# Edge layer: part of one term per block moved to ScalarE with a bias, and the correction sum formed in two steps

## The chip, the cores and the metric

The kernel runs on one core of one Trainium2 chip. The metric is the device time of one execution in microseconds. Each kernel is run several times and the median is compared. The core's engines run their own instruction streams side by side: PE (TensorE) multiplies matrices, DVE (VectorE), ACT (ScalarE) and POOL (GpSimd) work element by element, and SP issues transfers. SBUF is the on-chip memory, PSUM the small memory into which PE accumulates.

## The reference, cut to what matters

The program is a chain of four residual layers on a tensor of 4 images, 56 x 56 pixels, 128 channels. Each layer normalises its input by groups and adds its result to it. The change concerns layer 1 alone:

```python
def _L1_conv_ref(x, We, be, Wn, bn):
    f = x.shape[-1]
    W1, W2 = (We[:, :f], We[:, f:])
    proj_i = jnp.einsum('blnf,of->blno', x, W1)
    proj_j = jnp.einsum('blnf,of->blno', x, W2)
    edge = jax.nn.relu(proj_i[:, :, :, None, :] + proj_j[:, :, None, :, :] + be)
    edge_sum = edge.sum(axis=3)
    node_in = jnp.concatenate([x, edge_sum], axis=-1)
    node = jax.nn.relu(jnp.einsum('blnc,oc->blno', node_in, Wn) + bn)
    return node

x = x + _L1_conv_ref(_gn(x), L1_conv_We, L1_conv_be, L1_conv_Wn, L1_conv_bn)
```

For each image row l and each pixel n in it, the layer adds up relu(a[n] + b[m]) over all 56 pixels m of the same row, for 128 output channels. Here a is the first projection with its bias, and b the second. So there are 56 x 56 relus for each row and channel.

## The kernel before

The edge layer (`edge_layer`, from L1204) runs once for each image, between the attention and MLP of layer 0 for that image and the work that follows. Layers 2 and 3 come after all images, and the change doesn't touch them.

An image is cut into 7 blocks of 8 rows, that is 448 pixels (`NB`). The 56 pixels m are dealt out over the partitions: the 128 partitions hold 32 channels four times over, each time for another group of 14 pixels m, so that one "term" covers four pixels m at a time, and 14 terms (`M = HH // 4`) cover all 56. The 128 channels are cut into 4 quarters r of 32. A term is therefore a tile of 128 partitions x 4 quarters x 8 rows x 56 pixels, that is 128 x 1792 elements.

For each block, `project` lets PE compute four banks `e_pa` (first projection, one bank per quarter) and one bank `e_pc` (minus the second projection, 4 x 8 x 14 values). `evacuate` lets ACT copy them to SBUF as `e_a` (with the bias) and `e_c`, and adds the output bias to the residual. `normed` lets ACT normalise the input of the block after the next. With a in `e_a` and c = -b, the relu of a + b is relu(a - c), which is max(a, c) - c. Each term is made in one of three ways, by `terms` (L1265), which a string of one letter per term chooses:

- "d": DVE takes max(a, c) in one instruction (L1273), reading c from PSUM (`e_pc`). The missing "- c" is put in later, once for all d terms, by the correction.
- "p": POOL subtracts a - c (L1275), reading c from SBUF (`e_c`), and ACT applies the relu in place (L1277). No correction is needed.
- "s": a shared term. Quarters 0 and 1 are made as d, quarters 2 and 3 as p.

The letters stand in `EDGE_TURNS` for the first six blocks and in `EDGE_END` for the last. Before the change they are "ddpddpsdpdpddp" (8 d, 5 p, 1 s) and "ddpddpdpdpdddd" (10 d, 4 p).

PE then adds every term into the bank `e_acc`: four matmuls of 32 columns (L1344), one for each quarter, with a matrix that sums the four groups of partitions. The correction is a further set of four matmuls (L1360) with `e_rest`, which DVE makes by summing `e_c` over the d terms (L1366 and L1367). Where quarters 0 and 1 have one d term more than quarters 2 and 3, as with "s", the sum is taken in two instructions.

The order on PE, ACT and DVE is that of the program text (`tc.manual_schedule`). POOL's order is chosen by the framework from what the instructions depend on. In the text, at turn g the term is made and multiplied; then the finish of the block before last comes at g = 3 (`finish`, L1296, on DVE, which waits for PE's `e_po`), the first half of the next block's evacuation at g = 5, the second at g = 7, the sums for the correction at g = 8, the norm at g = 10 and the correction's matmuls at g = 11. After the last turn ACT copies the sums out of `e_acc` (L1369), and PE forms the output of the block before (`output`) and projects the block after the next.

Buffers: 7 tiles for d terms, 4 for p terms, 2 for each kind of partial tile. `e_a`, `e_c`, `e_rest` and `e_sums` have 2 each.

Of the kernel before, what the change touches and what calls it, by code (L numbers as in the profile page):

```python
# [12 lines left out]
F32 = mybir.dt.float32  # L13
AF = mybir.ActivationFunctionType
ALU = mybir.AluOpType
AX = mybir.AxisListType
# [3 lines left out]
P = 128  # L20
B = 4
HH = 56
# [10 lines left out]
def bc(ap, axis, n):  # L33

    ap = ap.unsqueeze(axis)
    shape = list(ap.shape)
    shape[axis] = n
    return ap.to_broadcast(shape)
# [1159 lines left out]

EDGE_TURNS, EDGE_END = "ddpddpsdpdpddp", "ddpddpdpdpdddd"


def edge_layer(k, w, x1, st):  # L1204
# [6 lines left out]
    nc, tc = k.nc, k.tc  # L1211
# [3 lines left out]
    with ExitStack() as es:  # L1215
        big = es.enter_context(tc.tile_pool(name="e_big", bufs=1))
        wk = es.enter_context(tc.tile_pool(name="e_wk", bufs=2))
# [7 lines left out]
        ready = {}  # L1225

        def normed(j):
            if j < 2:
                apply_norm(k, xg[:, blk(j)], xf[:, blk(j)], mr)
            elif j < NBLK:  # L1230
                nc.scalar.activation(xg[:, blk(j)], xf[:, blk(j)], AF.Identity, bias=shift, scale=mr[:, 1:2])
# [22 lines left out]
        def evacuate(j, part):  # L1254
            if j >= NBLK:
                return
            pc, pa, c, a = ready[j]
            for r in range(2 * part, 2 * part + 2):
                nc.scalar.activation(a[:, r, :], pa[r][:, :NB], AF.Identity, bias=w.be[:, r:r + 1])
                if r == 0:  # L1260
                    nc.scalar.copy(c.rearrange("p r l m -> p (r l m)"), pc[:, :NB])  # L1261
            if part == 1:
                nc.scalar.activation(xf[:, blk(j)], xf[:, blk(j)], AF.Identity, bias=w.bn)

        def terms(j, m, t, r0, r1, e):  # L1265

            pc, _, c, a = ready[j]
            if e == "d":
                c = pc[:, :NB].rearrange("p (r l m) -> p r l m", r=4, l=8)
            cm = bc(c[:, r0:r1, :, m], 3, HH)  # L1270
            am = a[:, r0:r1, :].rearrange("p r (l n) -> p r l n", l=8)
            if e == "d":
                nc.vector.tensor_tensor(t, am, cm, ALU.max)  # L1273
            else:
                nc.gpsimd.tensor_sub(t, am, cm)  # L1275
                tf = t.rearrange("p r l n -> p (r l n)")
                nc.scalar.activation(tf, tf, AF.Relu)  # L1277

        def tile_of(e, n=4):
            return wk.tile([P, n, 8, HH], F32, tag="e_%s%d" % (e, n), name="e_t" + e,  # L1280
                           bufs=2 if n < 4 else 7 if e == "d" else 4)
# [12 lines left out]
        def finish(j, po):  # L1294

            nc.vector.scalar_tensor_tensor(xf[:, blk(j)], po[:, :NB], w.nbn, xf[:, blk(j)], ALU.max, ALU.add)  # L1296

        with tc.manual_schedule(engines={mybir.EngineType.PE, mybir.EngineType.Activation, mybir.EngineType.DVE}):
            idle = psum.tile([P, 512], F32, tag="e_pc", name="e_idle", bufs=2)

            def fill(n):

                for _ in range(n):
                    nc.tensor.matmul(idle[:, :3 * P], k.ident, bc(k.ones, 1, 3), start=True, stop=True)
            mr = group_norm_factors(k, wk, bank, st, fill)
            nc.vector.tensor_scalar(shift, mr[:, 0:1], mr[:, 1:2], -1.0, ALU.mult, ALU.mult)
            for j in range(2):
                normed(j)
            project(0)
            for part in range(2):  # L1310
                evacuate(0, part)
            project(1)
            last = po = None
            for j in range(NBLK):
                end = j == NBLK - 1
                turns = EDGE_END if end else EDGE_TURNS
                nd, ns = turns.count("d"), turns.count("s")
                acc = psum.tile([P, 512], F32, name="e_acc")
                rest = wk.tile([P, 4, 8], F32, name="e_rest")
                at, ms = {"d": 0, "p": nd + ns, "s": nd}, []  # L1320
                for e in turns:
                    ms.append(at[e])
                    at[e] += 1
                early = {}
                if j == 0:
                    early = {g: tile_of(turns[g]) for g in
                             [g for g, e in enumerate(turns) if e == "d"][:3] + [turns.index("p")]}
                    for r in range(4):
                        for g, t in early.items():
                            terms(j, ms[g], t[:, r:r + 1], r, r + 1, turns[g])  # L1330
                for g, e in enumerate(turns):
                    m = ms[g]
                    if g in early:
                        parts = [(early[g], 0)]
                    elif e == "s":
                        parts = [(tile_of("d", 2), 0), (tile_of("p", 2), 2)]
                        for t, r in parts:
                            terms(j, m, t, r, r + 2, "p" if r else "d")
                    else:
                        parts = [(tile_of(e), 0)]  # L1340
                        terms(j, m, parts[0][0], 0, 4, e)
                    for t, r0 in parts:
                        for r in range(t.shape[1]):
                            nc.tensor.matmul(acc[quarters[r0 + r], :NB], w.S[:, 0, :], t[:, r].rearrange("p l n -> p (l n)"),  # L1344
                                             start=(g == 0), stop=(g == len(turns) - 1))
                    if g == 3 and po is not None:
                        finish(j - 2, po)
                    if g == 5:
                        evacuate(j + 1, 0)
                    if g == 7:  # L1350
                        evacuate(j + 1, 1)
                    if g == 10:
                        normed(j + 2)
                    if g == 6 and end:
                        po = output(*last)
                    if g == 9 and end:
                        finish(j - 1, po)
                    if g == 11:
                        for r in range(4):
                            nc.tensor.matmul(acc[quarters[r], :NB].rearrange("p (l n) -> p l n", l=8), w.S[:, 1, :],  # L1360
                                             bc(rest[:, r, :], 2, HH), start=False, stop=False)
                        if end:
                            po = begun(j)
                    if g == 8:
                        if ns:
                            nc.vector.tensor_reduce(rest[:, 0:2], ready[j][2][:, 0:2, :, 0:nd + 1], AX.X, ALU.add)  # L1366
                        nc.vector.tensor_reduce(rest[:, 2 if ns else 0:4], ready[j][2][:, 2 if ns else 0:4, :, 0:nd], AX.X, ALU.add)  # L1367
                sums = wk.tile([P, NB], F32, name="e_sums")
                nc.scalar.copy(sums, acc[:, :NB])  # L1369
                if end:  # L1370
                    idle = psum.tile([P, 512], F32, tag="e_pc", name="e_idle", bufs=2)
                    fill(2)
                if last and not end:
                    po = output(*last)
                project(j + 2)
                last = j, sums
            po = output(*last, po)
            fill(2)
            finish(NBLK - 1, po)
# [1476 lines left out]
def group_norm_factors(k, pool, bank, st, fill):  # L2856

    nc = k.nc
    mv = pool.tile([P, 2], F32, tag="mv", name="gf_mv")
    nc.vector.bn_aggr(mv, st.rearrange("p a b -> p (a b)"))  # L2860
    ps = bank()
    fill(2)
    nc.tensor.matmul(ps[:, 0:1], k.g4, mv[:, 0:1], start=True, stop=True)
    fill(1)
    mr = pool.tile([P, 2], F32, tag="mr", name="gf_mr")
    nc.vector.tensor_copy(mr[:, 0:1], ps[:, 0:1])
    t = pool.tile([P, 1], F32, tag="gt", name="gf_t")
    nc.vector.tensor_sub(t, mv[:, 0:1], mr[:, 0:1])
    nc.vector.tensor_mul(t, t, t)
    nc.vector.tensor_add(t, t, mv[:, 1:2])  # L2870
    ps = bank()
    nc.tensor.matmul(ps[:, 0:1], k.g4, t, start=True, stop=True)
    fill(1)
    nc.scalar.activation(t, ps[:, 0:1], AF.Sqrt, bias=k.eps)
    nc.vector.reciprocal(mr[:, 1:2], t)
    return mr
# [176 lines left out]
```

## Time and profile before

| | |
|---|---|
| median of 3 runs | 3447.18 us (3444.64 to 3448.79) |
| the profiled execution's own time | 3464.64 us |
| its span, first to last instruction | 3462.8 us |
| edge layer, first image: first DVE term | 544.46 us |
| edge layer, first image: end of the last DVE term | 673.31 us |
| starts of the sums copy (L1369), blocks 0 to 6 | 565.67, 583.91, 602.93, 620.73, 638.50, 655.72, 674.39 us |
| DVE, one whole term (L1273, 128 x 1792) | 2.01 us |
| POOL, one whole subtraction (L1275, 128 x 1792) | 3.28 us |
| POOL, two quarters / one quarter (L1275) | 1.74 / 0.95 us |
| ACT, relu of a whole term / two quarters / one quarter (L1277) | 1.71 / 0.96 / 0.57 us |
| DVE, the two correction sums (L1366, L1367) | 0.29, 0.27 us |

The four images' edge layers lie at about 541 to 677, 1175 to 1311, 1811 to 1947 and 2447 to 2583 us. Durations run from an instruction's start to its end. Instructions that follow each other on one engine overlap a little, so the time from start to start is shorter than the duration: a DVE term lasts 2.01 us, and the next starts 1.93 us after it.

### The profile page before, as it was taken

How to read it: one execution, taken by the hardware profiler on the slowest of the kernel's cores; microseconds unless marked ns; L12 is line 12 of the kernel's file. 1: busy time of each engine (PE TensorE's matmuls, PEld its weight loads, DVE VectorE, ACT ScalarE, POOL GpSimd, SP SyncE). 2: the span in 40 equal slices, each digit the busy share in tenths (PEclk: the TensorE clock that was granted, in tenths of full speed). 3: DMA queues.
4: the chain of work that ended last, by engine and by line, in shares of the span. 5: the costliest groups of instructions: out<-in, count | busy, mean ns of one | idle time of the engine just before them, and what ended most of it. 6: DMA issues, size and time to landing. Idle time of an engine off the chain costs nothing. (4 is left out here: it accounts for less than half of the span.)

```text
span 3462.8 us, 64536 instructions
## 1 busy us (share of the span) xinstructions
PE 3337.5 (96%) x27834; PEld 1441.2 (42%) x27834; DVE 2659.6 (77%) x2552; ACT 2134.9 (62%) x2257; POOL 1284.9 (37%) x795
## 2 busy tenths in 40 slices
PE   7999999999999999999999999999999999999998
PEld 4433333353333435333343443333337443346664
DVE  6588867868888696788859858887785878886756
ACT  4688876668888575788857568887654012215432
POOL 1000017700000490000019400001785978875766
PEclk9999999999999999999999999999999999999989
DMA  2243420024434000444310034342113057742201
GB/s 106 46 94 86 97 54 19 20 58 87 97 86 86 19 1 20 110 99 94 89 41 1 20 82 93 89 97 54 38 36 85 1 124 182 182 110 80 61 10 56
DMA packets 97868, 243.42 MB, mean 70 GB/s; under 512 B 64440, under 2 KB 69816, under 8 KB 92440
## 3 DMA queue, kind: packets, MB, share of 16 engines
q0 software_dynamic: 16128, 102.77, 14.8%
q1 hardware_dynamic: 74728, 123.61, 12.2%
q10 hardware_dynamic: 6720, 12.85, 1.3%
q8 instruction: 220, 3.60, 0.4%
q14 instruction: 72, 0.59, 0.1%
HBM read 79.43 MB, written 31.33 MB: 32 GB/s over the span
## 5 line engine op out<-in xcount | busy, mean ns | idle before, releaser
L830 ACT ACTIVATE f_ring<-f_pm 128x1792 f32<-128x1792 f32 (+1 forms) x764 | 1093.8, 1482 | 226.7 <-PE f_pm L827 179.2
L682 DVE TENSOR_TENSOR f_acc<-f_acc,f_ring 128x1792 f32<-128x1792 f32 x468 | 947.5, 2025 | 190.8 <-ACT f_ring L830 160.0
L827 PE MATMUL f_pm<-f_qT,f_kT 32*128 32x448 f32 x5376 | 722.8, 571 | 9.9 <-ACT f_p L716 4.1
L693 PE MATMUL f_pm<-f_ring,f_va 128*32 128x448 f32 (+1 forms) x6304 | 589.4, 490 | 0.0
L672 POOL DMA_DIRECT2D f_far<-f_ring x112 | 96.5, 862 | 1328.2 <-ACT f_ring L830 1027.0
L1275 POOL TENSOR_TENSOR e_tp<-e_a,e_c 128x1792 f32<-128x1792 f32 (+2 forms) x172 | 480.4, 2839 | 33.5 <-issue 33.4
L1273 DVE TENSOR_TENSOR e_td<-e_a,e_pc 128x1792 f32<-128x1792 f32 (+2 forms) x292 | 478.3, 1704 | 8.8 <-ACT e_c L1261 8.8
L827 PEld LDWEIGHTS f_pm<-f_qT,f_kT 32*128 32x128 f32 x5376 | 260.1, 183 | 411.8 <-ACT f_ring L830 301.1
L693 PEld LDWEIGHTS f_pm<-f_ring,f_va 128*32 128x32 f32 x6304 | 163.8, 109 | 410.1 <-issue 397.8
L1277 ACT ACTIVATE e_tp<-e_tp 128x1792 f32<-128x1792 f32 (+2 forms) x172 | 253.3, 1495 | 98.0 <-POOL e_tp L1275 98.0
L2040 DVE TENSOR_TENSOR u_ud<-u_px,u_d 112x1792 f32<-112x1792 f32 x144 | 263.4, 1863 | 39.9 <-PE u_po L2045 35.6
L2042 POOL TENSOR_TENSOR u_up<-xh,u_d 112x1792 f32<-112x1792 f32 (+1 forms) x72 | 240.9, 3374 | 56.0 <-PE u_po L2045 42.8
L1344 PE MATMUL e_acc<-e_td,t_edge 128*32 128x448 f32 x1952 | 231.6, 542 | 6.6 <-DVE e_td L1273 6.4
L2045 PE MATMUL u_po<-u_ud,AT 112*64 112x448 f32 x1056 | 212.4, 541 | 0.5 <-DVE u_ud L2040 0.5
L1344 PE MATMUL e_acc<-e_tp,t_edge 128*32 128x448 f32 x1184 | 148.0, 543 | 23.7 <-ACT e_tp L1277 23.6
L2045 PEld LDWEIGHTS u_po<-u_ud,AT 112*64 112x64 f32 x1056 | 74.0, 137 | 126.5 <-issue 112.3
L1344 PEld LDWEIGHTS e_acc<-e_td,t_edge 128*32 128x32 f32 x1952 | 61.8, 110 | 142.4 <-issue 94.2
L737 DVE RECIPROCAL f_den<-f_den 128x448 f32<-128x448 f32 x28 | 82.6, 2951 | 44.9 <-ACT f_den L734 44.9
L1874 POOL TENSOR_TENSOR q_u<-iS,q_g 128x1792 f32<-128x1792 f32 x32 | 104.3, 3287 | 12.2 <-PE q_acc L1889 12.2
L813 POOL TENSOR_TENSOR x<-xf,xw 128x343 f32<-128x343 f32 x28 | 25.5, 909 | 221.5 <-DVE xf L802 221.5
L2145 ACT COPY x_ev<-x_po 56x896 f32<-56x896 f32 x32 | 28.8, 900 | 126.7 <-DMA x_xs<-xat 57.8
L1889 PE MATMUL q_acc<-q_u,S 64*64 64x448 f32 x1024 | 101.2, 539 | 2.1 <-DVE y L1908 1.1
(538 smaller groups left out, 4622.3 us busy)
## 6 DMA issues: line engine op xcount, KB each, us to landing
f_far<-f_ring POOLq DMA_DIRECT2D x112, 896.0 KB, 6.4
u_d<-dd SPq DMA_DIRECT2D x46, 784.0 KB
f_far<-f_ring SPq DMA_DIRECT2D x28, 896.0 KB
xw<-in_x SPq DMA_DIRECT2D x4, 1568.0 KB
x2d<-x SPq DMA_DIRECT2D x4, 1568.0 KB
xat<-x SPq DMA_DIRECT2D x4, 1568.0 KB
x_xs<-xat ACTq DMA_DIRECT2D x32, 196.0 KB
xm<-x_ev ACTq DMA_DIRECT2D x64, 98.0 KB
```

The costliest lines, as they stand in the source:

```text
L682: nc.vector.tensor_add(e.acc, e.acc, slots(j, c))
L693: nc.tensor.matmul(e.po[heads[h], part], va[o, c, heads[h]], p, start=(c == 0), stop=(c == 23 and part.stop == NB))
L827: nc.tensor.matmul(ss[:, i, :NB], kT[heads[h], c * P:(c + 1) * P], qT[heads[h], blk(j)], start=True, stop=True)
L830: nc.scalar.activation(ring[:, slot:slot + m, :], ss[:, :m, :NB], AF.Exp, scale=scale)
L1273: nc.vector.tensor_tensor(t, am, cm, ALU.max)
L1275: nc.gpsimd.tensor_sub(t, am, cm)
L1277: nc.scalar.activation(tf, tf, AF.Relu)
L1344: nc.tensor.matmul(acc[quarters[r0 + r], :NB], w.S[:, 0, :], t[:, r].rearrange("p l n -> p (l n)"), start=(g == 0), stop=(g == len(turns) ...
L1874: nc.gpsimd.tensor_mul(u, bc(st.iS[:, bp, c, :HH], 1, HEADS), bc(g[:, n, c, :], 2, HH))
L2040: nc.vector.tensor_mul(u, bc(px[:, :, :NB], 2, m), dm)
L2042: nc.gpsimd.tensor_mul(u, bc(x, 2, m), dm)
L2045: nc.tensor.matmul(po[64 * b2:64 * b2 + 64, :NB], st.AT[:, 8 * i + h0 + q, 2 * bp + b2, :], u[:, b2, q, :], start=(left == 16), stop=(left ...
```

## The change

The letters become "ddpddpdpdpsddp" (still 8 d, 5 p, 1 s, with the s at turn 10 instead of 6) and, for the last block, "ddpddpdpdphddd" (9 d, 4 p, and one h at turn 10).

In a term "s" or "h", quarters 0 and 1 are now made by ACT alone: one activation for each of the 2 quarters x 8 rows, relu(a + bias) over 56 pixels, where the bias is a column of a small tile `e_less` that holds minus c. That makes 16 activations and one more for `e_less`, in four portions after turns 2, 4, 6 and 8. In "s", quarter 2 is made by DVE and quarter 3 by POOL and ACT. In "h", DVE makes quarters 2 and 3.

The correction is now one sum over the d terms for all four quarters, and one addition of the c of the shared term for the quarters that DVE made of it (one quarter in "s", two in "h").

```diff
-EDGE_TURNS, EDGE_END = "ddpddpsdpdpddp", "ddpddpdpdpdddd"
+EDGE_TURNS, EDGE_END = "ddpddpdpdpsddp", "ddpddpdpdphddd"
...
+        def singles(j, m):
+
+            t = tile_of("a", 2)
+            yield t
+            _, _, c, a = ready[j]
+            less = wk.tile([P, 2, 8], F32, name="e_less")
+            nc.scalar.activation(less, c[:, 0:2, :, m], AF.Identity, scale=-1.0)
+            for r in range(2):
+                for l in range(8):
+                    nc.scalar.activation(t[:, r, l, :], a[:, r, HH * l:HH * (l + 1)], AF.Relu, bias=less[:, r, l:l + 1])
+                    if l % 4 == 3:
+                        yield
...
-                nd, ns = turns.count("d"), turns.count("s")
+                nd, ns, nh = turns.count("d"), turns.count("s"), turns.count("h")
...
-                at, ms = {"d": 0, "p": nd + ns, "s": nd}, []
+                at, ms = {"d": 0, "p": nd + ns + nh, "s": nd, "h": nd}, []
...
+                work = singles(j, nd)
+                single = next(work)
...
-                    elif e == "s":
-                        parts = [(tile_of("d", 2), 0), (tile_of("p", 2), 2)]
-                        for t, r in parts:
-                            terms(j, m, t, r, r + 2, "p" if r else "d")
+                    elif e in "sh":
+                        parts = [(single, 0)]
+                        for e, r0, r1 in (("d", 2, 3), ("p", 3, 4)) if e == "s" else (("d", 2, 4),):
+                            parts.append((tile_of(e, r1 - r0), r0))
+                            terms(j, m, parts[-1][0], r0, r1, e)
...
+                    if g in (2, 4, 6, 8):
+                        next(work)
...
-                        if ns:
-                            nc.vector.tensor_reduce(rest[:, 0:2], ready[j][2][:, 0:2, :, 0:nd + 1], AX.X, ALU.add)
-                        nc.vector.tensor_reduce(rest[:, 2 if ns else 0:4], ready[j][2][:, 2 if ns else 0:4, :, 0:nd], AX.X, ALU.add)
+                        nc.vector.tensor_reduce(rest, ready[j][2][:, :, :, 0:nd], AX.X, ALU.add)
+                        r0, r1 = 2, 3 + nh
+                        nc.vector.tensor_add(rest[:, r0:r1], rest[:, r0:r1], ready[j][2][:, r0:r1, :, nd])
```

`ready[j][2]` is `e_c`, the copy of the second projection in SBUF.

## The prediction

> **What bounds the kernel now.** I read the page for shares, then busy time by stretch over the edge layer, then the timeline of each engine there.
>
> ```profile
> PE 3337.5 (96%) x27834; PEld 1441.2 (42%) x27834; DVE 2659.6 (77%) x2552; ACT 2134.9 (62%) x2257; POOL 1284.9 (37%) x795
> L1275 POOL TENSOR_TENSOR e_tp<-e_a,e_c 128x1792 f32<-128x1792 f32 (+2 forms) x172 | 480.4, 2839 | 33.5 <-issue 33.4
> L1273 DVE TENSOR_TENSOR e_td<-e_a,e_pc 128x1792 f32<-128x1792 f32 (+2 forms) x292 | 478.3, 1704 | 8.8 <-ACT e_c L1261 8.8
> ```
>
> The whole-span shares name PE, but the change lies in the edge layer alone, where POOL and DVE hardly rest (8.8 us of idle before 292 DVE terms). The next view is one steady block, then one image (columns: stretch, its length, busy us by engine).
>
> ```profile
> core 0: us, PE busy (x) PEld busy (x) DVE busy (x) ACT busy (x) POOL busy (x), PEclk, DMA share, GB/s
> 620.70:638.50 17.80, 17.46 (x165) 6.58 (x166) 17.53 (x13) 13.27 (x14) 17.80 (x7) 1.00 0.01 2
> 541.00:677.00 136.00, 127.92 (x1156) 46.22 (x1155) 127.07 (x97) 90.83 (x98) 120.41 (x45) 1.00 0.01 3
> ```
>
> PE's busy time here is waiting matmuls that overlap; four quarters follow the next four by 0.375 us, so a block needs about 9 us of it. POOL fills the block (17.80), DVE lacks 0.27 us, ACT has 4.5 us free. The timelines of POOL and DVE:
>
> ```profile
> 544.56 120.11 POOL L1275 TENSOR_TENSOR e_tp<-e_a,e_c 128x448 f32<-128x448 f32 x43 [8.32 <-issue]
> ...
> 622.40 0.68 DVE L1296 SCALAR_TENSOR_TENSOR x<-e_po,e_nbn,x 128x448 f32<-128x448 f32 x1 [0.27 <-PE e_po L1291]
> 623.00 4.94 DVE L1273 TENSOR_TENSOR e_td<-e_a,e_pc 128x1792 f32<-128x1792 f32 x3
> 627.86 0.29 DVE L1366 TENSOR_REDUCE e_rest<-e_c 128x16 f32<-128x144 f32 x1
> 628.08 0.28 DVE L1367 TENSOR_REDUCE e_rest<-e_c 128x16 f32<-128x128 f32 x1
> 628.27 11.66 DVE L1273 TENSOR_TENSOR e_td<-e_a,e_pc 128x1792 f32<-128x1792 f32 x6
> ...
> 676.60 0.68 DVE L1296 SCALAR_TENSOR_TENSOR x<-e_po,e_nbn,x 128x448 f32<-128x448 f32 x1 [3.29 <-PE e_po L1291]
> ```
>
> POOL runs 43 subtractions without a gap, but ends at 664.67, 9 us before DVE's last term (673.31). Over the image DVE is the chain: 128.85 us from 544.46 to 673.31, of which it waits 3.40 (0.96, 1.50, 0.27, 0.24 and 0.43, each before a finish). Its work is 125.45. POOL's pace and the finish waits add the rest.
>
> Start-to-start pitches: DVE term 1.93 (six in 11.66, the last lasting 2.01), half term 1.00 (the three in 4.94), quarter 0.53 (0.61 long less the same 0.08 overlap). POOL 3.22, half 1.68, quarter 0.91. ACT's relu of a whole term 1.60.
>
> **What the Trainium skill says.** "SBUF — State Buffer", section "Who interferes with whom": a DVE instruction with two SBUF inputs and a GpSimd instruction that reads SBUF exclude each other for the whole instruction, while a DVE instruction with one SBUF input, or a reduction, goes free. The trace agrees. DVE's terms read `e_a` in SBUF and `e_pc` in PSUM: 2.01 us with POOL full. The two reductions keep 0.27 to 0.30. But two SBUF inputs beside a POOL subtraction or product wait for its end (timeline elsewhere, and lines by source):
>
> ```profile
> 3203.47 3.28 DVE L2494 SCALAR_TENSOR_TENSOR o_f<-o_f,factors,o_e 128x7 f32<-128x7 f32 x1
> ...
> 3203.12 0.83 POOL L2568 TENSOR_TENSOR o_v<-o_v,o_dcs 128x392 f32<-128x392 f32 x1
> 3203.92 2.81 POOL L2539 TENSOR_TENSOR o_t<-o_t,o_f 128x1568 f32<-128x1568 f32 x1
> ```
>
> ```profile
> L1583 DVE TENSOR_TENSOR s_t<-s_mv,s_mr x4: 160/160/1579, 725.4 to 2615.5; 128x1 f32<-128x1 f32 x4
> L1643 ACT ACTIVATE s_d<-s_d,c_eps x4: 329/330/341, 747.7 to 2638.1; 128x56 f32<-128x56 f32 x4
> ```
>
> Seven elements took 3.28 us, to 0.02 after POOL's end at 3206.73; one element took 1.58 instead of 0.16. For short activations, "ScalarE: Activation LUTs", section "What ACT_TABLE_LOAD costs", states 280 ns + 0.833 per element with a pointer bias and an overlap of 93 ns: 327 for 56 elements. The trace has 330; the same overlap gives an estimated pitch of 0.233.
>
> **The change, part by part.**
> - DVE in the first six blocks: a half term becomes a quarter, 0.53 - 1.00 = -0.47. Two reductions (0.21 + 0.19) become one over 256 elements (between 274 ns at 128 and 473 at 320: about 0.41) and a dependent addition of 8 elements, 0.03 later and about 0.09 of pitch if alone: +0.12. Bare sum -0.35. End block: a term becomes a half, -0.93, and the addition +0.12. Per image 6 x -0.35 - 0.81 = -2.9: DVE work 122.55.
> - POOL: half becomes quarter, 1.68 - 0.91 = -0.77 a block; its cycle falls to 5 x 3.22 + 0.91 = 17.0.
> - ACT: adds `less` (0.235) and 16 activations at 0.233 (3.73), swaps a half relu (0.84) for a quarter (0.47). The four chunks stand in ACT's order before p1, p2, p3 and so before all that follows; what can't shrink is `sums` waiting for PE after the last relu (start to start 2.78, with 1.08 idle in every block). In pitches: sums 2.78 and its own 0.44, four relus 6.39, chunks 3.96, evacuations and bias 3.05, quarter 0.47, norm 0.67: 17.76. So ACT's slack is gone; it has just the cycle that POOL had. Between bounds: pitch 0.19 (no dearer than 7 elements in the trace) gives 17.1, no overlap (0.33) gives 19.3. I take 0.233.
> - PE: the same 56 quarter matmuls, in another order; nothing.
> - The addition `rest + c` reads two SBUF tiles. Before it nothing DVE does in the block needed that; POOL subtracts two SBUF tiles nearly all the time. Its wait is the rest of POOL's current instruction. Queued behind it on DVE are the quarter, d11, d12 and the next block's terms, and PE waits for them; POOL loses only some 0.1 us. Bounds: 0 (it arrives at a boundary) and 3.2 (just after one; the 3.28 row, which let one boundary pass, says this occurs). Without knowing the phase I take the mean of 0 to 3.2, 1.6. Not in the end block: POOL's last subtraction is over before.
>
> Sum: 122.55 + 6 x 1.6 = 132.15 against 128.85, +3.3 us an image, with no finish wait left (ACT's 17.76 is shorter than DVE's 17.1 + 1.6). All four images run this schedule and the next stage waits for their end (3.29 us from last term to last finish, unchanged): +13.2. The profiled execution is 3464.64 us (span 3462.8); the median is 3447.18, 0.5% less. The sum is carried over whole: **3460 us**.
>
> **Rivals.**
> 1. The additions meet POOL near its boundaries. DVE's work between two additions (17.0) is about POOL's cycle (17.0), so the phase tends to repeat and six cheap ones are possible; so are six dear ones. Then ACT's chain decides. Walked from the start, `sums` of block 0 comes 0.37 us earlier, of block 1 0.34, of blocks 2 to 4 about 1.65 (the trace has periods of 18.24, 19.02, 17.80, 17.77); block 5 has no norm, the end block saves DVE's half term: -3.3 us an image, -13: 3434. It decides where the waits sum to less than about 5 us an image, 0.8 a block. For it: POOL is 0.77 faster a block; against: uniform phases give twice that.
> 2. Waits of 5 to 8 us an image: 122.55 + 5 to 8 is 128 to 131, within 2 us of now: 3441 to 3455, centre 3447.
> 3. ACT's short runs don't overlap (0.33 each): cycle 19.3, 1.6 us over my 17.76 in about five blocks, -3.3 + 8 = +4.7 an image: 3466. Against: independent instructions overlap by 0.09 to 0.11 everywhere in ACT's timeline, whose shape is here:
>
> ```profile
> 617.95 1.70 ACT L1277 ACTIVATE e_tp<-e_tp 128x1792 f32<-128x1792 f32 x1 [1.92 <-POOL e_tp L1275]
> 620.73 0.53 ACT L1369 COPY e_sums<-e_acc 128x448 f32<-128x448 f32 x1 [1.08 <-PE e_acc L1344]
> 621.17 1.70 ACT L1277 ACTIVATE e_tp<-e_tp 128x1792 f32<-128x1792 f32 x1
> ```
>
> **How the numbers follow.** Forecast 0.50, rival 1 0.24, rival 2 0.17, rival 3 0.09. The forecast alone: waits of 1.4 to 2.6 a block give +2.1 to +9.3 an image, 3456 to 3484. The range reaches from rival 1's 3434 to 3482; below it lies half of rival 1 with a pitch under 0.23, above it waits near 2.6 and more. A measurement of this kernel tells about 0.2% (7 us) from no change. Slower: 0.48 of the forecast and rival 3's 0.09, 0.57. Faster: 0.23 of rival 1. The rest, 0.20, is the same.
>
> **What would show it.** In the changed trace the row of the addition: mean near 1.7 us with a spread of 0.2 to 3.3 in the first six blocks, 0.16 in the end block. A mean under 0.8 makes rival 1 right, and then DVE must show finish waits near 0.7 and ACT be without idle but for 1.1 before `sums`. The short activations: 0.33 long, pitch 0.23 (0.33 would be rival 3). POOL's quarter 0.95, and gaps in POOL where it runs out of tiles, since DVE's block takes 18.7. Wrong altogether if the edge stretch of an image (132.7 us from POOL's start to the end of the last finish) changes by something outside these rows.

## The result, and the profile after

The changed kernel takes 3512.39 us (3500.05 to 3516.07), the kernel before 3447.98 us beside it: the ratio is 1.0172, with an interval of 1.0153 to 1.0191. It is 1.7% slower. The forecast was 3460 us: slower, as said, but by about a fifth of the true amount, and the time lies outside the range.

The page after, in the same rows as before, and one row that is new:

```profile
PE 3336.8 (95%) x27834; PEld 1434.9 (41%) x27834; DVE 2724.5 (78%) x2556; ACT 2229.0 (64%) x2733; POOL 1267.3 (36%) x795
...
L1275 POOL TENSOR_TENSOR e_tp<-e_a,e_c 128x1792 f32<-128x1792 f32 (+1 forms) x172 | 462.5, 2729 | 86.5 <-ACT e_ta L1288 36.9
L1273 DVE TENSOR_TENSOR e_td<-e_a,e_pc 128x1792 f32<-128x1792 f32 (+2 forms) x292 | 463.3, 1651 | 8.8 <-ACT e_c L1261 8.8
...
L1288 ACT ACTIVATE e_ta<-e_a,e_less 128x56 f32<-128x56 f32 x448 | 113.0, 333 | 0.9
```

POOL's work fell from 480.4 to 462.5 us and DVE's terms from 478.3 to 463.3, as intended. But POOL now rests 86.5 us before its subtractions, where it rested 33.5, and DVE's total rose by 65 us (2659.6 to 2724.5) although its terms fell by 15. (An instruction that waits after it has begun counts as busy.) Busy time by stretch, one steady block and the whole first image:

```profile
core 0: us, PE busy (x) PEld busy (x) DVE busy (x) ACT busy (x) POOL busy (x), PEclk, DMA share, GB/s
616.00:634.80 18.80, 17.46 (x165) 6.64 (x166) 18.77 (x13) 16.64 (x32) 17.07 (x7) 1.00 0.01 2
541.00:694.00 153.00, 132.10 (x1155) 47.10 (x1155) 147.04 (x97) 114.29 (x217) 116.01 (x45) 0.94 0.01 2
```

A steady block takes 18.8 us instead of 17.8, and DVE is full, yet nothing was added to DVE but one short addition. The first image's granted clock is 0.94, where it was 1.00. DVE's timeline shows where it sits (the second block, then a steady one):

```profile
573.53 0.41 DVE L1383 TENSOR_REDUCE e_rest<-e_c 128x32 f32<-128x256 f32 x1
573.97 15.34 DVE L1385 TENSOR_TENSOR e_rest<-e_rest,e_c 128x8 f32<-128x8 f32 x1
...
625.30 0.41 DVE L1383 TENSOR_REDUCE e_rest<-e_c 128x32 f32<-128x256 f32 x1
625.74 1.84 DVE L1385 TENSOR_TENSOR e_rest<-e_rest,e_c 128x8 f32<-128x8 f32 x1
```

An addition of 8 elements took 1.84 us in one block and 15.34 us in another. POOL's timeline beside the long one, and POOL's next instruction:

```profile
569.03 20.25 POOL L1275 TENSOR_TENSOR e_tp<-e_a,e_c 128x1792 f32<-128x1792 f32 x7
...
597.32 3.26 POOL L1275 TENSOR_TENSOR e_tp<-e_a,e_c 128x1792 f32<-128x1792 f32 x1 [8.04 <-PE e_acc L1362]
```

These are the last seven subtractions of an unbroken run, which ended at 589.28. The addition stood ready from 573.97, was passed over at five boundaries between them, and ended at 589.31. POOL had stopped because it then waited 8.04 us for PE, and PE in turn had waited 6.04 us for the DVE terms queued behind the addition. So the long wait ended only when it had brought POOL itself to a halt. By source, all 28 additions and all short activations:

```profile
L1385 DVE TENSOR_TENSOR e_rest<-e_rest,e_c x28: 185/1836/15342, 556.7 to 2618.5; 128x8 f32<-128x8 f32 x24, 128x16 f32<-128x16 f32 x4
...
L1288 ACT ACTIVATE e_ta<-e_a,e_less x448: 324/331/352, 549.2 to 2617.6; 128x56 f32<-128x56 f32 x150
```

(minimum, median and maximum in ns). The long one occurs twice, in the second block of images 1 and 2. The other 22 additions of the first six blocks were let in at POOL's first boundary.

**Where the time lies.** From the first DVE term to the end of the last finish, the four images take 150.15, 149.97, 139.15 and 140.66 us, 579.9 together. Before they took 132.8 each, 531.3: +48.6 us. Another 12.3 us comes after the last image, outside the edge layer: from its last finish to POOL's first `q_u` (the next large product on POOL, L1892) it takes 90.5 us, and before 78.2. The span of the profiled execution of before hides this second part, as the experiments show. Images 1 and 2, with the long addition, are some 10 us longer than 3 and 4.

### The profile page after: what moved, and what is told of

It reads as the page before. It is cut to its first block, busy times and chain, and to the rows that moved or that the text cites. A ratio compares the mean times of both kernels' runs of the same rounds, so it can differ in the third digit from the quotient of the medians.

```text
span 3510.0 us, 64909 instructions
## 1 busy us (share of the span) xinstructions
PE 3336.8 (95%) x27834; PEld 1434.9 (41%) x27834; DVE 2724.5 (78%) x2556; ACT 2229.0 (64%) x2733; POOL 1267.3 (36%) x795
## 5 line engine op out<-in xcount | busy, mean ns | idle before, releaser
L1275 POOL TENSOR_TENSOR e_tp<-e_a,e_c 128x1792 f32<-128x1792 f32 (+1 forms) x172 | 462.5, 2729 | 86.5 <-ACT e_ta L1288 36.9
L1273 DVE TENSOR_TENSOR e_td<-e_a,e_pc 128x1792 f32<-128x1792 f32 (+2 forms) x292 | 463.3, 1651 | 8.8 <-ACT e_c L1261 8.8
L1277 ACT ACTIVATE e_tp<-e_tp 128x1792 f32<-128x1792 f32 (+1 forms) x172 | 242.3, 1434 | 0.3
L1288 ACT ACTIVATE e_ta<-e_a,e_less 128x56 f32<-128x56 f32 x448 | 113.0, 333 | 0.9
L1892 POOL TENSOR_TENSOR q_u<-iS,q_g 128x1792 f32<-128x1792 f32 x32 | 104.3, 3289 | 12.6 <-PE q_acc L1907 12.6
```

The source lines that it names most:

```text
L1288: nc.scalar.activation(t[:, r, l, :], a[:, r, HH * l:HH * (l + 1)], AF.Relu, bias=less[:, r, l:l + 1])
```

## The experiments

The theory after the first reading: two things cost time, and each can be removed alone. The addition waits for POOL, and the short activations, put ahead of the relus, delay the terms that PE waits for. The rivals were that one of the two explains it all. The stage after the last image was taken up later (from 8 on).

**1. The addition reads PSUM.** It takes c from `e_pc`, so that it has one input in SBUF.

```diff
-                        nc.vector.tensor_add(rest[:, r0:r1], rest[:, r0:r1], ready[j][2][:, r0:r1, :, nd])
+                        pcv = ready[j][0][:, :NB].rearrange("p (r l m) -> p r l m", r=4, l=8)
+                        nc.vector.tensor_add(rest[:, r0:r1], rest[:, r0:r1], pcv[:, r0:r1, :, nd])
```

> The changed kernel, but the addition of the correction reads the shared term's c from PSUM (e_pc) instead of its SBUF copy (e_c), so that it has one SBUF input; all else stays. Lock theory (the loss is the addition waiting for POOL): the addition takes under 0.25 us in every block, no wait of DVE on POOL is left, and the time falls from 3512 to 3428 to 3442 us, a little under the kernel before (ACT's cycle of 17.76 us then sets the block). ACT theory (the loss is the 17 short activations in ACT's queue, with the waits and the halved PE clock that they bring): the addition gets short, but blocks stay near 18.8 us and the time over 3480 us.

3482.88 us, ratio 1.0094 (1.0079 to 1.0109). The row of the addition now:

```profile
L1386 DVE TENSOR_TENSOR e_rest<-e_rest,e_pc x28: 161/163/171, 555.5 to 2591.7; 128x8 f32<-128x8 f32 x24, 128x16 f32<-128x16 f32 x4
```

Every wait is gone, and with it 0.8% of the time. But the blocks still take 18.77 us from one sums copy to the next, as they did in the changed kernel. The addition is about half of the loss, and something else holds the same period. The images now take 139.76, 138.05, 140.12 and 139.76 us: the first two lost 10.4 and 11.9 us, and the last two, where six waits of usual length had summed to about 11 us, stayed within 1 us of what they were. So the two long additions are the whole cost of the addition in these two traces; waits of 1 to 3 us cost nothing here, because the block lasts 18.77 us without them too.

**2. The addition alone.** The kernel before, with one sum over the d terms and an addition from SBUF for quarters 0 and 1, and no short activations.

```diff
-                            nc.vector.tensor_reduce(rest[:, 0:2], ready[j][2][:, 0:2, :, 0:nd + 1], AX.X, ALU.add)
-                        nc.vector.tensor_reduce(rest[:, 2 if ns else 0:4], ready[j][2][:, 2 if ns else 0:4, :, 0:nd], AX.X, ALU.add)
+                            nc.vector.tensor_add(rest[:, 0:2], rest[:, 0:2], ready[j][2][:, 0:2, :, nd])
...
+                        nc.vector.tensor_reduce(rest, ready[j][2][:, :, :, 0:nd], AX.X, ALU.add)
```

> The kernel before with one part of the change alone: its letters and halves stay, no activations row by row, but the correction is one sum over the d terms and an SBUF + SBUF addition for quarters 0 and 1. Lock theory: the addition waits 0.1 to 3.3 us per block, sometimes through several subtractions, mean at least 1.6 us in the first six blocks; DVE work of 125.45 us an image + 0.7 + 9.6 or more is 6 us or more above now, so 3465 to 3515 us. ACT theory: within 0.2% of 3448 us.

3485.26 us (3468.03 to 3496.49), ratio 1.0097 (1.0080 to 1.0114), with images of 135.38, 152.90, 135.30 and 145.01 us. DVE and POOL around the worst addition:

```profile
1226.00 14.92 DVE L1367 TENSOR_TENSOR e_rest<-e_rest,e_c 128x16 f32<-128x16 f32 x1
```

```profile
1214.96 25.91 POOL L1275 TENSOR_TENSOR e_tp<-e_a,e_c 128x896 f32<-128x896 f32 x9
```

Again the addition ends (1240.92) only where POOL's unbroken run does (1240.87). In the same kernel other additions took 0.33, 0.98 or 2.52 us, and one in image 4 took 10.04. So one addition of 16 elements a block costs 1% by itself. Most of it lies in the two images with a long one, which are 20.1 and 12.2 us longer than before; the other two are 2.5 us longer.

**3. Its control.** The same with c from PSUM (the edit of experiment 1 on experiment 2).

> The block of before, with one reduction over the d terms and the addition for quarters 0 and 1, which reads c from PSUM, and no short activations. If the exclusion of two SBUF readers is all that the addition costs: additions of 0.16 to 0.19 us, periods and total of before, 3450 (3443 to 3457). If the dependent pair of instructions itself costs DVE's chain something (0.1 to 0.3 us a block): 3453 to 3462. If the order of the reduction matters as much as the exclusion: near the 3485 of the addition from SBUF.

3450.51 us, ratio 1.0000 (0.9989 to 1.0010), additions of 0.17 us and the periods of before. The sum in two steps costs nothing that can be measured; all of experiment 2's loss is the second SBUF input.

**4. No addition at all.** In the changed kernel POOL makes quarter 2 of the shared term and DVE quarter 3, so that two reductions do the correction.

```diff
-                        for e, r0, r1 in (("d", 2, 3), ("p", 3, 4)) if e == "s" else (("d", 2, 4),):
+                        for e, r0, r1 in (("p", 2, 3), ("d", 3, 4)) if e == "s" else (("d", 2, 4),):
...
-                        nc.vector.tensor_reduce(rest, ready[j][2][:, :, :, 0:nd], AX.X, ALU.add)
-                        r0, r1 = 2, 3 + nh
-                        nc.vector.tensor_add(rest[:, r0:r1], rest[:, r0:r1], ready[j][2][:, r0:r1, :, nd])
+                        r0 = 2 if nh else 3
+                        nc.vector.tensor_reduce(rest[:, 0:r0], ready[j][2][:, 0:r0, :, 0:nd], AX.X, ALU.add)
+                        nc.vector.tensor_reduce(rest[:, r0:4], ready[j][2][:, r0:4, :, 0:nd + 1], AX.X, ALU.add)
```

> The changed kernel with the correction formed by two reductions instead of a reduction and an addition: in the shared term POOL makes quarter 2 and DVE quarter 3, so that quarters 0 to 2 are summed over the d terms and quarter 3 over one more. Lock theory: no DVE instruction with two SBUF inputs is left, time as with the PSUM addition to 0.2% (3428 to 3442 us). ACT theory: over 3480 us.

3488.66 us, ratio 1.0113 (1.0098 to 1.0128), period 18.77: no better than experiment 1. The rest of the loss isn't in the correction.

**5. One relu for the sixteen activations.** Experiment 1 with a single relu of 896 elements after turn 8. It leaves out the subtraction of c in these two quarters.

```diff
-            for r in range(2):
-                for l in range(8):
-                    nc.scalar.activation(t[:, r, l, :], a[:, r, HH * l:HH * (l + 1)], AF.Relu, bias=less[:, r, l:l + 1])
-                    if l % 4 == 3:
-                        yield
+            for i in range(4):
+                if i == 3:
+                    nc.scalar.activation(t.rearrange("p r l n -> p (r l n)"), a[:, 0:2, :].rearrange("p r n -> p (r n)"), AF.Relu)
+                yield
```

> The variant with the PSUM addition, and in place of the 16 activations with a bias one plain relu over the two quarters (896 elements, after turn 8); it leaves out the subtraction of c for these two quarters, so ACT has 0.84 us a block there instead of 3.73. If ACT's chain sets the block once the lock is gone, the time falls below the PSUM addition's by 1.5 to 3 us an image, 6 to 12 us, to 3418 to 3430 us, with DVE's 17.1 us a block as the bound. If ACT's short runs cost nothing beyond what is hidden, the two agree to 0.1%. If the ACT theory is right, this one is near 3430 us while the PSUM addition stays over 3480 us.

3448.10 us, ratio 0.9993 (0.9985 to 1.0001), period 17.22. The period fell as expected, but the total missed the expected 3418 to 3430 by 18 us; experiments 8 and 9 find most of these in the stage after the last image. The activations are the other half. But is it their sum (3.7 us a block) or their place? The changed kernel's ACT and PE, from one sums copy to the next PE chain:

```profile
615.98 0.53 ACT L1387 COPY e_sums<-e_acc 128x448 f32<-128x448 f32 x1 [2.12 <-PE e_acc L1362]
616.41 1.70 ACT L1277 ACTIVATE e_tp<-e_tp 128x1792 f32<-128x1792 f32 x1
618.01 0.22 ACT L1285 ACTIVATE e_less<-e_c 128x16 f32<-128x16 f32 x1
618.26 1.97 ACT L1288 ACTIVATE e_ta<-e_a,e_less 128x56 f32<-128x56 f32 x8
620.14 1.68 ACT L1277 ACTIVATE e_tp<-e_tp 128x1792 f32<-128x1792 f32 x1
...
623.18 1.03 ACT L1288 ACTIVATE e_ta<-e_a,e_less 128x56 f32<-128x56 f32 x4
624.11 1.69 ACT L1277 ACTIVATE e_tp<-e_tp 128x1792 f32<-128x1792 f32 x1
...
627.29 1.04 ACT L1288 ACTIVATE e_ta<-e_a,e_less 128x56 f32<-128x56 f32 x4
628.22 2.16 ACT L1277 ACTIVATE e_tp<-e_tp 128x1792 f32<-128x1792 f32 x2
```

```profile
611.20 0.96 PE L1362 MATMUL e_acc<-e_tp,t_edge 128*32 128x448 f32 x8 [1.35 <-ACT e_tp L1277]
...
612.73 0.93 PE L1362 MATMUL e_acc<-e_td,t_edge 128*32 128x448 f32 x8
613.48 0.94 PE L1378 MATMUL e_acc<-e_rest,t_edge 128*32 128x448 f32 x8
614.23 0.94 PE L1362 MATMUL e_acc<-e_td,t_edge 128*32 128x448 f32 x8
614.98 0.93 PE L1362 MATMUL e_acc<-e_tp,t_edge 128*32 128x448 f32 x8
...
629.97 0.96 PE L1362 MATMUL e_acc<-e_tp,t_edge 128*32 128x448 f32 x8 [1.34 <-ACT e_tp L1277]
```

PE waits for the relu of p3, the last but one of the five whole p terms p0 to p4 (at 611.20 and 629.97). From there six sets of matmuls follow each other by 0.75 us, and sums can be copied at 615.98, 4.78 us later. From sums ACT works without a pause to the end of p3's relu, all 16 activations included, until PE takes it up at 629.97: 13.99 us. Together 18.77, the period measured. ACT's idle before sums (2.12 us) is no reserve: it stands after the last activation, not ahead of p3.

**6. Half of them moved.** Experiment 1, with eight of the next block's activations put between p4's relu and sums.

```diff
-                work = singles(j, nd)
-                single = next(work)
+                if j == 0:
+                    work = singles(j, nd)
+                    single = next(work)
+                slots, following = (2, 4, 6, 8) if j == 0 else (2, 4), None
...
-                    if g in (2, 4, 6, 8):
+                    if g in slots:
...
+                    if g == 13 and not end:
+                        work = singles(j + 1, (EDGE_END if j + 1 == NBLK - 1 else EDGE_TURNS).count("d"))
+                        following = next(work)
+                        for _ in range(2):
+                            next(work)
...
+                single = following or single
```

> Addition reads PSUM, all 16 short activations stay, but eight of them (for the next block) stand between the relu of p4 and sums, where ScalarE waits 2.1 us for PE, instead of between the relus of p1 to p3. Theory of the loop (sums to the end of p3's relu 13.93 us on ScalarE, then 4.84 us on PE to the next sums): 13.93 - 1.86 + 4.84 = 16.9, so PE's own 17.22 becomes the period, the images fall to 128 to 131 us and the total to about 3450 (3445 to 3458). Rival, that ScalarE's sum of work makes the period wherever it stands: 18.77 stays and 3483 with it.

3446.24 us, ratio 0.9986 (0.9978 to 0.9994). Period 17.22, images 127.8 to 129.5 us. A steady block, and ACT at its end:

```profile
600.00:617.20 17.20, 17.20 (x168) 6.67 (x164) 17.13 (x13) 16.60 (x31) 17.06 (x7) 1.00 0.01 2
```

```profile
614.86 1.97 ACT L1288 ACTIVATE e_ta<-e_a,e_less 128x56 f32<-128x56 f32 x8
617.41 0.54 ACT L1395 COPY e_sums<-e_acc 128x448 f32<-128x448 f32 x1 [0.59 <-PE e_acc L1369]
```

ACT works as long as in the changed kernel (16.60 against 16.64 us), and the block is 1.55 us shorter. So the place was the cost, not the sum. Now all four engines are nearly full, and PE has no gap.

**7. Is PE then the bound?** Experiment 5 with the matmuls of its fifth term issued twice (that term counts twice).

```diff
-                    for t, r0 in parts:
+                    for t, r0 in parts + (parts if g == 4 else []):
```

> The kernel with one plain relu in place of the 16 short activations (it leaves out the subtraction of c in two quarters of that term), and the matmuls of the fifth term of each block issued twice, so that this term counts twice. Eight records of 0.094 us more a block. If PE is the bound of these blocks (17.22 us, of which 15 terms of 0.75): period 17.97, 5.3 us an image, +21 us: 3469. If PE needs only about 9 us a block, as my prediction took it: 17.22 and 3448 stay.

3462.14 us, ratio 1.0037 (1.0023 to 1.0050). The period is 17.97, exactly 0.75 more, and the images 131.67 to 131.92, 13 us together above experiment 5's. PE needs the whole block, at least in this variant. The total rose by 14 us and not by 21: the four periods of the middle grew by 0.75 each and the last by 0.55, but the first didn't grow (16.5 to 17.9 us, beside 16.3 to 19.6).

**8. What the rest hides.** The edge layer of experiment 6 is 16.7 us shorter than that of before (514.6 against 531.3), but its time only about 4 us. The kernel before was therefore profiled again.

> The kernel before, profiled a second time. If the first profile's edge layer (132.8 us an image, blocks of 17.80 us) is what this kernel always does: 132.8 again, to 0.3 us, and a total near 3450. If that execution was an unusual one, whose total of 3464.6 stood 17 us over the median: an edge layer of about 128.5 us an image (17 us / 4 = 4.3 less) and no finish waits over 1 us.

Its images take 132.8 us again, so the edge layer is what it is; the profiled execution took 3452.08 us. The first one, of 3464.64, had a stretch of 34.1 us at half the TensorE clock late in the program (from 3303 us), the second one of 17.1 us (from 3277). That accounts for most of the 17 us by which the first profile stood over its median, far from the change: from the first `q_u` to the end it took 801.1 us, and 785.7 in the trace of experiment 3, which has no such stretch. What is missing is found in the stage after the last image. Transfers issued by SyncE, and POOL, in the changed kernel (its last finish ends at 2630.34):

```profile
2630.83 1.28 SPq L158 DMA_DIRECT2D t_w_qk<-in_w_qk  x1
2638.13 0.32 SPq L3009 DMA_DIRECT2D xw<-xad  x1
2638.49 0.43 SPq L158 DMA_DIRECT2D t_w_qk<-in_w_qk  x1
2644.19 0.32 SPq L3009 DMA_DIRECT2D xw<-xad  x1
2644.57 0.41 SPq L158 DMA_DIRECT2D t_w_qkr<-in_w_qkr  x1
```

```profile
2648.49 0.25 POOL L1806 TENSOR_TENSOR t_w_qk<-t_w_qk,t_w_qkr 128x32 f32<-128x32 f32 x1 [9.20 <-DMA t_w_qkr<-in_w_qkr]
```

And in the kernel before (last finish 2583.57):

```profile
2583.02 0.95 SPq L158 DMA_DIRECT2D t_w_qk<-in_w_qk  x2
2584.01 1.00 SPq L158 DMA_DIRECT2D t_w_qkr<-in_w_qkr  x1
2591.53 0.33 SPq L2991 DMA_DIRECT2D xw<-xad  x1
```

In the changed kernel two loads of `xw`, issued only 7.3 and 5.7 us after the transfers ahead of them, stand before the weights `t_w_qkr` in SyncE's queue. These are issued 14.2 us after the last finish instead of 0.4, and POOL's chain behind them waits.

That chain is not what `q_u` waits for. POOL has done its part long before and stands idle for 39.9 us (39.1 before) until PE releases it, and PE is the busiest engine of this stretch (72.8 of 78.2 us before). But POOL's late work now lies beside the statistics that DVE makes for PE. First the second step of these before, then both steps, PE and POOL in the changed kernel:

```profile
2617.09 0.23 DVE L1584 SCALAR_TENSOR_TENSOR s_t<-s_t,s_mv 128x1 f32<-128x1 f32 x1
```

```profile
2660.87 3.14 DVE L1601 TENSOR_TENSOR s_t<-s_mv,s_mr 128x1 f32<-128x1 f32 x1
2664.04 7.73 DVE L1602 SCALAR_TENSOR_TENSOR s_t<-s_t,s_mv 128x1 f32<-128x1 f32 x1
...
2671.83 0.59 PE L1606 MATMUL s_pt<-s_t,t_shared 128*128 128x1 f32 x2 [9.21 <-DVE s_t L1602]
...
2720.61 0.22 POOL L1859 TENSOR_TENSOR q_ww<-t_images 128x16 f32<-128x16 f32 x1 [39.88 <-PE s_px L1722]
```

Steps of one element with two SBUF inputs wait here as the addition did, and PE waits 9.21 us for them. (No run gave these steps an operand from PSUM; that it is the same exclusion is argued from their inputs and from POOL's work beside them.) PE's idle time between the last finish and `q_u` grew from 5.4 to 14.8 us, 9.4 of the 12.3. During that wait the granted clock halved, for 13.65 us, where the same stretch of before has 3.41 us of half clock; that is the likely remainder. The experiments without the short activations (2 and 3) have the old order, with `q_u` 76 to 79 us after the last finish and 5 to 6 us of idle PE; those with their tile (1 and 4 to 7) have the new one, 91 to 93 us and 13 to 16. The suspect is SBUF: the tile `e_ta` and three kinds of partial tiles take 21,504 bytes of a partition where before took 14,336 (2 buffers each of 1,792 bytes a quarter).

**9. The footprint alone.** The kernel before with 7,168 bytes more.

```diff
-                              bufs=2 if n < 4 else 7 if e == "d" else 4)
+                              bufs=(4 if e == "p" else 2) if n < 4 else 7 if e == "d" else 4)
```

> The kernel before with one number changed: four buffers instead of two for POOL's half term, 7,168 bytes of a partition more, as much as the change adds. No instruction of the edge layer differs. Theory of the layout: edge layer 132.8 us an image as before, q_u after the last image at 91 to 93 us instead of 78, 3450 + 15 = 3465 (3460 to 3468). Rival: 3450.

3461.51 us, ratio 1.0050 (1.0034 to 1.0066). Images of 132.8 us as before, `q_u` at 93.3 us, and the queue and DVE's statistics in the new way (last finish 2580.72):

```profile
2588.35 0.32 SPq L2991 DMA_DIRECT2D xw<-xad  x1
2588.71 0.43 SPq L158 DMA_DIRECT2D t_w_qk<-in_w_qk  x1
2597.65 0.32 SPq L2991 DMA_DIRECT2D xw<-xad  x1
2598.03 0.41 SPq L158 DMA_DIRECT2D t_w_qkr<-in_w_qkr  x1
```

Two of DVE's steps on the statistics take 4.16 and 7.41 us here, and PE is idle for 13.2 us. The bytes of two buffers cost 0.5%, in a stage that the edit doesn't touch. Why they change the order of the queue was not traced, and no size between 14,336 and 21,504 bytes was tried.

**10. The changed kernel with a small footprint.** One buffer for the short activations' tile, none of its own for the half term of the end block: 10,752 bytes.

```diff
-                              bufs=2 if n < 4 else 7 if e == "d" else 4)
+                              bufs=1 if e == "a" else 2 if n < 4 else 7 if e == "d" else 4)
...
-                            parts.append((tile_of(e, r1 - r0), r0))
+                            parts.append((tile_of(e, r1 - r0) if ns else tile_of(e)[:, 0:2], r0))
```

> The changed kernel itself with the small footprint (one buffer for the short activations' tile, none of its own for the half term). Theory: edge layer as in the changed kernel (139 to 150 us an image), stage after it 15 us earlier: 3512 - 15 = 3497 (3487 to 3503; the starved additions vary). Rival: 3512 stays.

3488.80 us (3480.75 to 3507.38), ratio 1.0113 (1.0098 to 1.0128), `q_u` at 78.0 us. The median lies below the expected 3497 but inside its range. The profiled execution, at 3507.38 the longest of five, had the 15.3 us additions in three images instead of two. If their number varies from one execution to the next, that explains the spread and the low median; with one execution traced, this is not shown.

**11. All three removed.** Experiment 6 with the edit of experiment 10.

> The kernel with moved activations and PSUM addition, but with one buffer instead of two for the tile of the short activations and no buffers of its own for the half term of the end block: 10,752 bytes of a partition for the partial tiles, where before had 14,336 and the change 21,504. Theory of the layout: with the small footprint SyncE's queue again issues the loads of t_w_qk and t_w_qkr ahead of xw's after the last image, POOL's chain there starts some 15 us earlier (q_u from 92.9 to about 78 us after the last finish), edge layer unchanged (128 to 129.5 us an image): 3446 - 15 = 3431 (3425 to 3436), below the kernel before by 0.5%. Rival, that the 15 us come from something else in the changed edge layer: q_u stays at 92.9 and 3446 stays.

3425.53 us (3424.34 to 3432.05) beside 3444.94 for the kernel before: ratio 0.9943 (0.9930 to 0.9956). `q_u` comes 78.9 us after the last finish. SyncE's queue there (last finish 2563.57):

```profile
2563.02 0.93 SPq L158 DMA_DIRECT2D t_w_qk<-in_w_qk  x2
2563.99 0.95 SPq L158 DMA_DIRECT2D t_w_qkr<-in_w_qkr  x1
```

This is faster than both kernels. The idea of the change was good for 0.57%; of the 19.4 us, 16.7 are found in the edge layer (514.6 us against 531.3). From the ratios of the runs, what buried it, with the costs taken off in this order (in another order the shares shift a little: the footprint alone cost 0.50% in experiment 9):

| step | ratios | per cent | us at 3447 |
|---|---|---|---|
| the change without its three costs | 0.9943 | -0.57 | -20 |
| larger footprint (6 against 11) | 0.9943 to 0.9986 | +0.43 | +15 |
| eight activations ahead of p3 (1 against 6) | 0.9986 to 1.0094 | +1.08 | +37 |
| addition from SBUF (changed kernel against 1) | 1.0094 to 1.0172 | +0.78 | +27 |

## Why the prediction was wrong

**The direction** was right, and in part by luck: the largest cost, 37 us for the place of the activations, was put at nothing, and the waits that made up the forecast cost nothing where they had the forecast's length. Part of the reason was right. The exclusion of two SBUF readers, which the Trainium skill states ("SBUF — State Buffer", section "Who interferes with whom"), was put on the right instruction. Its median in the trace is 1.84 us, where 1.6 was taken; the mean of the first six blocks is 2.98. The other prices held: a short activation 0.331 us (0.33) with a pitch of 0.232 (0.233), which agrees with the estimate from "ScalarE: Activation LUTs", section "What ACT_TABLE_LOAD costs"; the reduction 0.406 (0.41); the end block's addition 0.19 (0.16). And POOL did run into gaps.

**The failed step of PE.** "PE's busy time here is waiting matmuls that overlap; four quarters follow the next four by 0.375 us, so a block needs about 9 us of it." The lines show a term as eight records, not four, and full terms 0.75 us apart. Fifteen such sets are 11.25 us; projections and output fill the rest of 17.2. Experiment 7 shows it: one term more, 0.75 us more. "PE: the same 56 quarter matmuls, in another order; nothing" fell with it: experiments 1 and 6 have the same matmuls, and PE waits 1.35 us a block for the relu of p3 in experiment 1 and not at all in 6.

**The failed step of ACT.** "So ACT's slack is gone; it has just the cycle that POOL had", 17.76. The sum of pitches was right: ACT is busy 16.64 us in the measured block, and with the 1.08 of idle that is 17.72. The error was to take that idle as fixed and at the last relu. With p3's relu late, sums waits for six sets of matmuls behind p3, and the loop is 13.99 + 4.78 = 18.77. Experiment 6 shows it by moving eight activations and nothing else. The same delay leaves PE idle in the first block, and then its clock falls:

```profile
556.94 0.96 PE L1362 MATMUL e_acc<-e_tp,t_edge 128*32 128x448 f32 x8 [1.51 <-ACT e_tp L1277]
...
561.05 0.96 PE L1362 MATMUL e_acc<-e_tp,t_edge 128*32 128x448 f32 x8 [2.40 <-ACT e_tp L1277]
...
563.17 1.74 PE L1362 MATMUL e_acc<-e_td,t_edge 128*32 128x448 f32 x8
```

The eight records of a term take 1.74 us there instead of 0.94. Each of the first two images has 17.1 us of half clock (13.65 of them around the long addition, during which PE was idle for 6.04 us), the last two 3.4 and 6.8, where the edge layer of before had none. What the half clock adds by itself was not separated.

**The bound of the wait.** "Bounds: 0 (it arrives at a boundary) and 3.2 (just after one...)". The additions of the first six blocks sum to 24.6 us in image 1, with 15.34 in one of them, and to about 11 in images 3 and 4, against 9.6 taken for the waits. The 3.28 us row of before "let one boundary pass"; the prediction read it as the worst case, where it was a sign that boundaries can be passed at all. Rival 1 needed waits below 5 us an image and was out of reach. The sum itself failed too: "122.55 + 6 x 1.6 = 132.15" lays the waits end to end on DVE's work as if DVE were the path. Images 3 and 4 have the waits and take 139.15 and 140.66 us, and experiment 1 has none and takes 138.05 to 140.12: the loop of ACT and PE is the path, and it hides them.

**What was left out.** "... the next stage waits for their end (3.29 us from last term to last finish, unchanged)": these 3.29 us did stay, but the stage behind them was put at nothing. It lost 12.3 us in the traces (15 to 17 us of the time in experiments 9 and 11), because the larger footprint moved POOL's work beside DVE's statistics, where the same exclusion seems to act again. The new tile's buffers appear nowhere in the sum. The first profile also hid it: its 17 us over the median lay in a stretch of half clock that had nothing to do with the change, so that the two spans differ by 47 us where the medians differ by 64.

## What to carry to other kernels

Where several engines are nearly full in a stage, price a change by the loop that passes through them, from a copy to the instruction that the next copy depends on: work placed ahead of that instruction costs its length, the same work behind it may cost nothing. On DVE a scrap of an instruction with two SBUF inputs, beside back-to-back work of POOL, can't be priced at one POOL instruction: it may wait until POOL stops. Give it an operand from PSUM. And count every new tile against the stages that follow: bytes alone can reorder their transfers, and with them what runs beside what.

## What the runs showed of the hardware that was not expected

- A DVE instruction with two SBUF inputs isn't always served at POOL's next boundary. In the traces of the changed kernel and of experiments 2 and 10 it was let in at the first boundary 65 times of 72, and passed over 7 times. Each of these 7 waits (10.04 to 15.35 us) ended within 0.05 us of the end of POOL's unbroken run, and POOL then waited 5.4 to 8.1 us for PE. What decides between the two was not found. It isn't the phase: in the second block the addition came 1.55 us before the end of POOL's subtraction in all four images of the changed kernel, and was passed over in two and let in in two. In the stage after the last image, a one-element step of DVE took 0.23 us before and 7.73 us in the changed kernel, beside a run of short POOL instructions.
- The granted clock halved for 3.4 us after PE had been idle 1.51 and then, within 4 us, 2.40 us. The Trainium skill ("TensorE: Matmul & The Clock Gate", section "HAM oscillation — how this bites in real kernels") gives idle gaps above about 3.4 us as the rule; here shorter gaps close together were followed by it. The length of the stretches, 3.4 us and multiples, agrees with the window of 3413 ns that the same page states (section "What's actually happening").
